# Block 0's input in 128-token halves, a split last product, gates by token in blocks 4 to 7, and block 3's statistics taken earlier

## The chip, the cores and the metric

The kernel runs on one core of one Trainium2 chip, in one launch. The metric is device time in microseconds (us), the median of several executions; before the change it is 523.41 us (three runs, 523.15 to 523.43). Each kernel also has one profiled execution, whose span is counted from its first to its last recorded instruction. In profile lines, PE is the matrix engine (TensorE), PEld its weight loads, DVE the vector engine, ACT the scalar engine, POOL the GpSimd engine, SP the sync engine, which here issues DMAs; a "q" behind a name is that engine's instruction queue.

## What is computed

The input is x, 2048 tokens of 256 channels in f32. Two sublayers stand in a sandwich: the input of each is normalised, and so is what it gives before it is added.

```python
x = x + layernorm(long_block(layernorm(x), ...))
x = x + layernorm(moe(layernorm(x), ...))

# long_block(x): 16 heads of 16 channels
h      = layernorm(x) * ln1w + ln1b
x_conv = silu(causal_depthwise_conv4(h) + conv_b)
q, k   = l2norm(h @ Wq), l2norm(h @ Wk)
v      = layernorm_per_head(h @ Wv) * vnw + vnb
i_gate = sigmoid(x_conv @ Wig + big)            # 256 wide
gamma  = sigmoid(x_conv @ Wg + bg)              # one per head, 16 wide
mem    = scan over tokens: mem[t] = gamma[t] * mem[t-1] + i_gate[t] * k[t] * v[t]
out    = groupnorm(layernorm_per_head(mem) * q) * sigmoid(x_conv @ Wog + bog)
h      = x + out @ Wo
return h + (silu(h2 @ Wgate) * (h2 @ Wval)) @ Wout      # h2 = layernorm(h), FF 1024

# moe(x): 8 experts of width 176, top 2, and a shared expert of width 704
routed + sigmoid(x @ shared_gate_w) * shared(x)
```

## The kernel before

The tokens are cut into 8 blocks of 256 (`TB`), each block into two halves of 128 tokens (`NT`), the channels into two halves of 128 (`KC`). "By token" means that tokens lie on the 128 partitions, "by channel" that channels do; PE transposes (line 380) go from one to the other. A block passes through these steps, each a small function:

- `enter` (lines 400 to 430): `enter_stats` takes bn_stats and bn_aggr of x on DVE (lines 322, 323) and on POOL `va` (line 410) and the root `inner` (line 411); `enter_norm` makes `ln_nb` on DVE (line 341) and normalises on ACT (line 343). These serve two nested norms in one. `enter_back` keeps what undoes the norm.
- `project` (lines 432 to 594): `hT` transposes the normed block and evicts it on ACT (line 447) with ln1w and ln1b as scale and bias; `conv` works as matmuls with diagonal matrices; `k`, `v` and `q` are products by token; `vscale`, `vk` finish v on DVE (lines 532 to 535, 538); `gate_in` and `gate_out` are products by channel with a tanh on ACT (line 552); `decay` is a product onto 16 rows, one for each head, a tanh, and a DMA that spreads each row over the 16 channels of its head. Every product is recorded on line 389.
- `remember` (lines 596 to 652): `scan` transposes v to channels, multiplies it by (tanh + 1) (line 606) and runs the recurrence (line 611); then `memT`, `msum`, `oscale`, `oq`, `osum`, `onorm`.
- `leave` (lines 654 to 700), `perceptron` (lines 702 to 737, 8 chunks of the hidden width, evicted on lines 724 and 725), `route` (lines 758 to 847), the shared expert (lines 854 to 882), then 36 routed blocks of 128 rows (lines 944 to 995).

Three things set the order of the work. A list written out by hand, `opening` (lines 1075 to 1087), names the steps of the first blocks one after another; each is issued behind what DVE, POOL, ACT and PE have so far. After it, `places` gives each remaining step a place, 8 places to a block, and the steps of all blocks are issued sorted by place, perceptron chunks between them. A second list by hand, `closing` (lines 1191 to 1201), orders combination, final norms and the late shared products of blocks 5 to 7; 7.6 there is the last product, of block 7's second half of tokens, and the two L steps are the two parts of `finish_last` (line 1029), whose small operations go to POOL by `scale_of` (lines 333, 334). Within the order issued, a tile scheduler places semaphores; each engine executes its own instructions in order.

PSUM is 8 banks by name: psA has two, psM three, psB, psS and psD one each (line 68). A product or a set of transposes takes one, and the next user of the bank waits until it was read.

At the start, x is loaded on SP's queue, then the weights, w_k, w_v and so on; four small rows (ln1w, ln1b, conv_b, conv_w) are loaded on ACT's queue. PE meanwhile runs ten matmuls of 512 columns on zeros (`warm_up`, line 150); two calls of `stay_warm`, six short matmuls each, stand beside hT's transposes. `vector_columns` turns the three rows into columns on PE (line 232) and a copy (line 235).

Of the kernel before, what the change touches and what calls it, by code (L numbers as in the profile page):

```python
# [27 lines left out]
def kernel(ctx: ExitStack, tc: tile.TileContext, a: dict, out: bass.AP):  # L28
# [93 lines left out]
    def load_x(b):  # L122
        x_tiles[b] = act.tile([P, NT, C], F32, tag="x", name=f"x_{b}", bufs=NB)
        nc.sync.dma_start(x_tiles[b], in_tokens(x, b))

    def in_rows(ap):
        return ap.rearrange("(k p) n -> p k n", p=P)
# [23 lines left out]

    warm_up(10)
    loads = ExitStack()
# [8 lines left out]
    nc.sync.dma_start(w_v, in_rows(a["Wv"]))  # L162
    w_io = att.tile([P, KC, 2 * C], F32, name="w_io")
    nc.sync.dma_start(w_io[:, :, 0:C], in_rows(a["Wig"]))
    head_rows = {nm: const.tile([P, D], F32, name=nm) for nm in ("vnw", "vnb", "mnw", "mnb")}
    loads.close()
    load_x(1)
    w_g = const.tile([P, KC, H], F32, name="w_g")
    nc.sync.dma_start(w_g, in_rows(a["Wg"]))
# [9 lines left out]
    nc.sync.dma_start(w_qk[:, :, 0:C], in_rows(a["Wq"]))  # L179
    nc.sync.dma_start(w_io[:, :, C:], in_rows(a["Wog"]))  # L180

# [75 lines left out]
    w_g_wide = act.tile([P, KC, C], F32, tag="f", name="w_g_wide", bufs=NB)  # L257

    wv_sum = const.tile([P, KC * H], F32, name="wv_sum")
    wv_heads = w_v.rearrange("p k (h d) -> p (k h) d", d=D)  # L260
# [55 lines left out]

    def stats(part, src):
        nt = src.shape[1]
        st = small.tile([P, nt, 6], F32, tag=f"st{part}", name="ln_st")
        mv = small.tile([P, nt, 2], F32, tag=f"mv{part}", name="ln_mv", bufs=6)  # L320
        for n in range(nt):
            nc.vector.bn_stats(st[:, n, :], src[:, n, :])  # L322
            nc.vector.bn_aggr(mv[:, n, :], st[:, n, :])  # L323
        return mv

# [74 lines left out]
    def enter(b):  # L400

        t, xt = live[b], x_tiles[b]

        def enter_stats():


            mv = stats("L", xt)
            inner = small.tile([P, NT], F32, tag="inner", name=f"inner_{b}", bufs=3)
            va = small.tile([P, NT], F32, tag="va", name=f"va_{b}", bufs=3)
            nc.gpsimd.tensor_scalar(va, mv[:, :, 1], 1.0 + EPS, EPS * EPS, ALU.mult, ALU.add)  # L410
            nc.gpsimd.tensor_tensor(inner, va, neg_half, ALU.pow)
            t.update(mv=mv, inner=inner, va=va)

        def enter_back():

            mv, inner, va = t["mv"], t["inner"], t["va"]
            outer = small.tile([P, NT], F32, tag="outer", name=f"outer_{b}")
            nc.gpsimd.tensor_scalar(outer, mv[:, :, 1], EPS, None, ALU.add)
            nc.gpsimd.tensor_tensor(outer, outer, neg_half, ALU.pow)
            back = small.tile([P, NT], F32, tag="back", name=f"back_{b}", bufs=5)  # L420
            nc.gpsimd.tensor_tensor(back, va, inner, ALU.mult)
            nc.gpsimd.tensor_tensor(back, back, outer, ALU.mult)
            t.update(back=back)

        def enter_norm():
            ln = att.tile([P, NT, C], F32, tag="ln1", name=f"ln1_{b}", bufs=4)
            normalize("L", ln, xt, t["mv"], t["inner"])
            t.update(ln=ln)

        return enter_stats, enter_back, enter_norm  # L430

    def project(b):
# [6 lines left out]
        def hT():  # L439
            hT_ = att.tile([P, KC, HALO + TB], F32, tag="hT", name=f"hT_{b}", bufs=3)  # L440
            if halo[0] is None:
                nc.gpsimd.memset(hT_[:, :, 0:HALO], 0.0)
            else:
                nc.gpsimd.tensor_copy(hT_[:, :, 0:HALO], halo[0][:, :, TB : TB + HALO])
            pt = to_channels(next(banks), t["ln"])
            for k in range(KC):
                nc.scalar.activation(
                    hT_[:, k, HALO:], pt[:, k, :], AF.Identity, bias=ln1b[k], scale=ln1w[k]
                )
            halo[0] = t["hT"] = hT_  # L450
# [86 lines left out]
        def vk():  # L537
            nc.vector.tensor_tensor(t["v"], t["v"], t["k"], ALU.mult)


# [19 lines left out]
        def decay():  # L560
# [15 lines left out]

            product(po[0:H, 0:TB], [w_g[:, k, :] for k in range(KC)], xc)
            by_head = att.tile([H, TB], F32, tag="by_head", name=f"by_head_{b}", bufs=2)
# [12 lines left out]
            values("q", w_qk[:, :, 0:C], 3), qsum, vscale, vk,  # L591
            gate("gate_in", w_io, 0, big_h, 2), decay,
            gate("gate_out", w_io, C, bog_h, 4),
        )

    def remember(b):
# [7 lines left out]
        def scan():  # L604
            u = t["gate_in"]
            nc.vector.scalar_tensor_tensor(
                u, u, 1.0, to_channels(bank, t["v"]), ALU.add, ALU.mult
            )
            mem = att.tile([P, KC, TB], F32, tag="mem", name=f"mem_{b}", bufs=2)
            for k in range(KC):  # L610
                nc.vector.tensor_tensor_scan(  # L611
                    mem[:, k, :], t["decay"][:, k, :], u[:, k, :],
                    0.0 if last[0] is None else last[0][:, k, TB - 1 : TB], ALU.mult, ALU.add,
                )
            last[0] = t["mem"] = mem
# [236 lines left out]
    all_banks = cycle("MAMDBMAS")  # L852

    def shared(b, banks=cycle("S"), shid=shid):

# [13 lines left out]
        f_ = part_of[b] if b >= LATE_FROM else new_part(b)  # L869
        for n in range(NT):  # L870
            pn = psum(next(banks))[:, 0:C]
            product(
                pn, [shid[:, f, tok(n)] for f in range(NS)], [s_down[:, f, :] for f in range(NS)],
            )
            gate = t["gate"][:, n : n + 1]
            if b < LATE_FROM:
                nc.scalar.activation(f_[:, n, :], pn, AF.Copy, scale=gate)
            else:
                nc.vector.scalar_tensor_tensor(
                    f_[:, n, :], pn, gate, f_[:, n, :], ALU.mult, ALU.add  # L880
                )
            yield
# [146 lines left out]
    def finish_last(b, n):  # L1029

        f_ = part_of[b][:, n : n + 1, :]
        mv, rs = scale_of("R", f_)
        nc.vector.tensor_scalar(f_[:, 0, :], f_[:, 0, :], mv[:, 0, 0:1], None, ALU.subtract)
        yield
# [8 lines left out]
    def evenly(n):  # L1043
# [4 lines left out]
        "hT": 0.2, "tap0": 0.3, "silu": 0.31, "k": 1.2, "ksum": 1.21, "v": 1.4, "vsum": 1.41, "vroot": 1.42, "conv": 0.3,  # L1048
        "q": 2.2, "qsum": 2.21, "vscale": 3.3, "vk": 4.3, "gate_in": 3.5, "decay": 4.5,
        "gate_out": 5.5,  # L1050
# [18 lines left out]
    for run in (  # L1069
# [11 lines left out]
        gate_in:1 qsum:1 osum decay:1 onorm gate_out:1 k:2 way_out_columns oT vroot:1 ksum:2 v:2 enter_back:1  # L1081
        h1 q:2 ln2_stats vsum:2 ln2_norm vscale:1 vk:1 conv:2 h2T enter_back:2 tables_ready
    """
# [96 lines left out]
    for b in range(LATE_FROM, NB):  # L1180
# [12 lines left out]
        6.2 N0 C2 5.6 X0 A2 6.3 A5 N1 C3 6.4 X1 A3 C6 7.0 N2 N5 C4 6.5 X2 A4 7.1 N3 X5 6.6 A6 X3 C7  # L1193
        7.2 N4 7.3 X4 N6 7.4 X6 7.5 L0 7.6 L1 L0 L1
    """
# [39 lines left out]
```

## Time and profile before

| | before |
|---|---|
| median of three runs | 523.41 us (523.15 to 523.43) |
| profiled execution | 523.42 us, its span 521.3, granted PE clock 0.996 |
| first product of k begins | 8.11 us |
| last matmul ends, last DVE operation ends | 511.48, 514.47 us |
| PE busy, 0 to 8.1 us | 5.89 us, mostly `warm_up` and `stay_warm` |
| PE busy, 60 to 65 us | 4.04 of 5 us |
| gate product onto 16 rows, blocks 4 to 7 | four records each, 0.96 us on PE |
| `gate_in` product, 8 records | 1.72 to 1.73 us on PE |

The longest waits of PE, from the trace's list of waits (engine, tile, line, whom it waited for: sum in us, times, longest):

```profile
PE psA L380 <- ACT ln L343: 1.6, 3, 1.0
PE psD L150 <- DVE cold L145: 1.2, 1, 1.2
PE psB L380 <- ACT ln L343: 0.5, 1, 0.5
PE psB L380 <- DVE o L650: 0.5, 1, 0.5
```

How to read the views below. A page gives for each engine its busy time, the share of the span and the number of instructions. A table of stretches gives for each stretch of the span its length, the busy time of PE, PEld, DVE, ACT and POOL with numbers of instructions, the granted PE clock (1.00 is full), the mean share of the 16 DMA engines and GB/s. A chain of waits is followed back from a last instruction: start, length, engine, tile and line. A timeline line gives start, busy time, engine, line, operation, out<-in, shapes and, in brackets, the idle time before it and who ended that. Matmul records are pipelined, so the busy time of a group is longer than from its start to the next group's start; a 128x256 f32 product is passed in 0.216 us a record.

### The profile page before, as it was taken

The page shows a single profiled execution, that of the slowest core. Times are in us where ns is not written, and L with a number is a line of the kernel's source. Part 1 is how long each engine was busy: PE and PEld are TensorE (multiplying, and loading weights), DVE is VectorE, ACT ScalarE, POOL GpSimd, SP SyncE. Part 2 cuts the span into 40 slices and gives each one's busy share as a digit, 9 for nine tenths or more (in the row PEclk, how much of TensorE's full clock was granted, in tenths as well). Part 3 has the DMA queues.
Part 4 walks back from the last instruction along what each step waited for, and adds up shares of the span by engine and source line. Part 5 has one row for each costly group of instructions (what it writes and reads, how often), then busy time and mean ns, then how long its engine had stood idle before and what let it go on. Part 6 is the DMA issues. An engine that isn't in the chain of part 4 may idle for free.

```text
span 521.3 us, 7930 instructions
## 1 busy us (share of the span) xinstructions
PE 505.0 (97%) x2468; PEld 421.7 (81%) x2468; DVE 331.7 (64%) x1100; ACT 217.5 (42%) x500; POOL 169.6 (33%) x309
## 2 busy tenths in 40 slices
PE   8999899999999999999999999999999999999992
PEld 5877687888888888888888888888877777778881
DVE  4788999888797896997764233235144444441983
ACT  4665463544544635643343322222134444443250
POOL 7233202213243342412426013035003443332551
PEclk9999999999999999999999999999999999999998
DMA  4991101001011011110103901003614433423621
GB/s 116 386 297 22 20 2 20 1 1 20 2 55 21 14 40 22 40 28 7 55 1 117 306 5 54 1 7 123 166 29 130 119 109 113 118 75 132 249 94 49
DMA packets 31792, 41.26 MB, mean 79 GB/s; under 512 B 4824, under 2 KB 26628, under 8 KB 31750
## 3 DMA queue, kind: packets, MB, share of 16 engines
q1 hardware_dynamic: 27888, 30.96, 20.5%
q0 software_dynamic: 3584, 9.79, 5.7%
q8 instruction: 20, 0.33, 0.3%
q14 instruction: 22, 0.18, 0.1%
q10 hardware_dynamic: 278, 0.01, 0.0%
HBM read 24.28 MB, written 15.15 MB: 76 GB/s over the span
## 4 chain that ended last, share of the span: by engine, by line
PE 82%; DVE 12%; POOL 2%; issue 1%; ACT 1%; DMA 1%; POOLq 0%; DVEq 0%
PE psM L389 35%; PE psA L389 17%; PE psD L714 9%; PE psD L389 7%; PE psS L389 5%; PE psB L389 3%; PE psA L952 2%; PE psB L980 2%; DVE ln_st L322 1%; DVE mem L611 1%; PE psB L380 1%; POOL ln_rs L334 1%; DVE hid L725 1%; DVE sm L373 1%; PE psM L380 1%
## 5 line engine op out<-in xcount | busy, mean ns | idle before, releaser
L389 PE MATMUL psM<-h2T,w_gate 128*128 128x256 f32 x256 | 66.6, 382 | 0.0
L389 PE MATMUL psM<-h2T,w_val 128*128 128x256 f32 x256 | 66.0, 379 | 0.0
L714 PE MATMUL psD<-w_out,hid 128*128 128x256 f32 x256 | 64.2, 380 | 0.1
L991 POOL DMA_INDIRECT ys<-yb,pair x36 | 35.5, 985 | 74.5 <-ACT yb L990 73.2
L389 PEld LDWEIGHTS psM<-h2T,w_gate 128*128 128x128 f32 x256 | 47.6, 190 | 8.2 <-DVE o L635 1.3
L714 PEld LDWEIGHTS psD<-w_out,hid 128*128 128x128 f32 x256 | 48.2, 190 | 7.3 <-DVE hid L725 1.0
L389 PEld LDWEIGHTS psM<-h2T,w_val 128*128 128x128 f32 x256 | 48.5, 190 | 6.5
L389 PE MATMUL psM<-m_w,xT 128*128 x144 | 48.7, 460 | 0.3 <-issue 0.3
L724 ACT ACTIVATE hid<-psM 128x256 f32<-128x256 f32 x64 | 23.8, 377 | 50.0 <-PE psM L389 49.8
L333 POOL TENSOR_SCALAR ln_rs<-ln_mv 128x2 f32<-128x2 f32 (+1 forms) x33 | 8.6, 260 | 106.5 <-DVE ln_mv L323 92.7
L725 DVE TENSOR_TENSOR hid<-hid,psM 128x256 f32<-128x256 f32 x64 | 26.1, 411 | 24.8 <-ACT hid L724 24.4
L842 POOL DMA_INDIRECT xs<-ln,rows x32 | 32.3, 1010 | 15.7 <-issue 7.2
L389 PE MATMUL psD<-m_w,hT 128*128 x144 | 37.2, 381 | 0.0
L389 PEld LDWEIGHTS psM<-m_w,xT 128*128 128x128 f32 x144 | 24.6, 190 | 8.2 <-issue 0.6
L389 PE MATMUL psA<-yT,s_gu 128*128 128x256 f32 x128 | 30.8, 381 | 0.0
L954 DVE COPY xT<-psA 128x256 f32<-128x256 f32 x36 | 15.3, 424 | 24.1 <-PE psA L952 24.1
L976 DVE TENSOR_TENSOR xb<-xb,psM 128x176 f32<-128x176 f32 x36 | 12.2, 338 | 27.0 <-ACT xb L975 17.2
L334 POOL TENSOR_TENSOR ln_rs<-ln_rs,neg_half 128x2 f32<-128x2 f32 (+1 forms) x33 | 25.8, 782 | 2.2
L389 PEld LDWEIGHTS psD<-m_w,hT 128*128 128x128 f32 x144 | 24.5, 190 | 2.4 <-ACT yb L990 0.5
L389 PEld LDWEIGHTS psA<-yT,s_gu 128*128 128x128 f32 x128 | 23.9, 190 | 3.0
L975 ACT ACTIVATE xb<-psM 128x176 f32<-128x176 f32 x36 | 11.4, 318 | 32.7 <-PE psM L389 31.8
L990 ACT ACTIVATE yb<-psD,share 128x256 f32<-128x256 f32 x36 | 17.1, 474 | 18.5 <-PE psD L389 18.4
(269 smaller groups left out, 1062.4 us busy)
## 6 DMA issues: line engine op xcount, KB each, us to landing
xb<-xs SPq DMA_DIRECT2D x36, 169.5 KB
g<-ys SPq DMA_DIRECT2D x8, 512.0 KB
xs<-zeros SPq DMA_DIRECT2D x16, 169.5 KB
x<-in_L_attn_x_dram SPq DMA_DIRECT2D x8, 256.0 KB
decay<-by_head SPq DMA_DIRECT2D x14, 128.0 KB
out_dram<-f SPq DMA_DIRECT2D x7, 256.0 KB
m_w<-in_L_ffn_w_gate_dram SPq DMA_DIRECT2D x2, 704.0 KB
m_w<-in_L_ffn_w_up_dram SPq DMA_DIRECT2D x2, 704.0 KB
```

Of the source, the lines that this page charges most:

```text
L334: roots.append(nc.gpsimd.tensor_tensor(rs, rs, neg_half[:, 0:nt], ALU.pow).ins)
L380: nc.tensor.transpose(pt[:, k * TB + n * P : k * TB + (n + 1) * P], src[:, n, k * P : (k + 1) * P], ident,)
L389: nc.tensor.matmul(po, lhs[i], rhs[i], start=(i == 0), stop=(i == len(lhs) - 1))
L714: nc.tensor.matmul(total[:, n * C : (n + 1) * C], hids[f][:, tok(n)], w_out[:, f, :], start=(f == 0 and n == 0), stop=(f == NF - 1 and n = ...
L724: nc.scalar.activation(hid, po[:, 0:TB], AF.Silu)
L725: nc.vector.tensor_tensor(hid, hid, po[:, TB:], ALU.mult)
L842: inst = nc.gpsimd.indirect_dma_start(out=xs, out_offset=bass.IndirectOffsetOnAxis(ap=rows[:, c : c + 1], axis=0), in_=ln[:, n, :], in_off ...
L954: nc.vector.tensor_copy(xT, pt[:, 0 : KC * P].rearrange("p (k t) -> p k t", k=KC))
L975: nc.scalar.activation(h[:, 0:I], po[:, 0:I], AF.Silu)
L976: nc.vector.tensor_tensor(h[:, 0:I], h[:, 0:I], po[:, I:GU], ALU.mult)
L990: nc.scalar.activation(yb, po[:, 0:C], AF.Copy, scale=share)
L991: inst = nc.gpsimd.indirect_dma_start(out=ys, out_offset=bass.IndirectOffsetOnAxis(ap=pair, axis=0), in_=yb, in_offset=None, bounds_check= ...
```

## The change

- Block 0's x is loaded as two DMAs of 128 tokens, the first on SP's queue, the second on ACT's queue (ahead of the four small rows). Its statistics, `va`, `inner`, `ln_nb`, norm, transposes and eviction go half by half; of the evictions, channel half 0 stays on ACT and channel half 1 goes to DVE. `warm_up` runs nine matmuls instead of ten.
- `w_io` holds Wig, Wg and Wog side by side. For blocks 4 to 7, `gate_in` is a product by token, 272 columns wide, of Wig and Wg together: the convolved tokens are the stationary side. ACT copies it out of two psA banks, DVE adds the row `big` (loaded over all partitions at the start), ACT takes the tanh. `vk` then multiplies by (tanh + 1) by token, so `scan` reads the transposed product straight from PSUM. `decay` transposes the 16 columns of Wg's part to 16 rows instead of making a product. The places of `gate_in` and `decay` go from 3.5 to 3.8 and from 4.5 to 5.0 in all blocks.
- `enter_stats` of block 3 leaves its place and goes into `opening`, between `vscale:1` and `vk:1`.
- In `closing`, the last product is made in two halves of 128 output channels, each evicted and taken into bn_stats by itself. For both halves of tokens, `finish_last` adds epsilon on DVE instead of POOL; the root stays on POOL.

On each engine this moves, beside the operations named: on POOL, block 0's `va` and `inner` become four operations on one column each, in the order va, va, inner, inner; on ACT, the DMAs of conv_b and conv_w wait for the semaphores of the two x halves; on PE, block 0's transposes fill a psA and a psM bank.

```diff
     def load_x(b):
         x_tiles[b] = act.tile([P, NT, C], F32, tag="x", name=f"x_{b}", bufs=NB)
-        nc.sync.dma_start(x_tiles[b], in_tokens(x, b))
+        if b > 0:
+            nc.sync.dma_start(x_tiles[b], in_tokens(x, b))
+        else:
+            for n, queue in enumerate((nc.sync, nc.scalar)):
+                queue.dma_start(x_tiles[b][:, n, :], in_tokens(x, b)[:, n, :])
...
-    warm_up(10)
+    warm_up(9)
...
-    w_io = att.tile([P, KC, 2 * C], F32, name="w_io")
+    w_io = att.tile([P, KC, 2 * C + H], F32, name="w_io")
...
-    w_g = const.tile([P, KC, H], F32, name="w_g")
+    w_g = w_io[:, :, C : C + H]
...
+    BY_TOKEN = tuple(range(4, NB))
+    big_row = act.tile([P, NT, C], F32, tag="f", name="big_row", bufs=NB)[:, 0, :]
+    nc.sync.dma_start(big_row, a["big"].partition_broadcast(P))
...
         def enter_stats():
-            mv = stats("L", xt)
             inner = small.tile([P, NT], F32, tag="inner", name=f"inner_{b}", bufs=3)
             va = small.tile([P, NT], F32, tag="va", name=f"va_{b}", bufs=3)
-            nc.gpsimd.tensor_scalar(va, mv[:, :, 1], 1.0 + EPS, EPS * EPS, ALU.mult, ALU.add)
-            nc.gpsimd.tensor_tensor(inner, va, neg_half, ALU.pow)
+            def root(ns, mv):
+                nc.gpsimd.tensor_scalar(
+                    va[:, ns], mv[:, ns, 1], 1.0 + EPS, EPS * EPS, ALU.mult, ALU.add
+                )
+                nc.gpsimd.tensor_tensor(inner[:, ns], va[:, ns], neg_half[:, ns], ALU.pow)
+            if b > 0:
+                mv = stats("L", xt)
+                root(slice(0, NT), mv)
+            else:
+                mv = stats("L", xt, lambda n, mv: root(slice(n, n + 1), mv))
...
         def enter_norm():
-            normalize("L", ln, xt, t["mv"], t["inner"])
+            for ns in [slice(0, NT)] if b > 0 else [slice(n, n + 1) for n in range(NT)]:
+                normalize("L", ln[:, ns, :], xt[:, ns, :], t["mv"][:, ns, :], t["inner"][:, ns])
...
+                for n in range(NT):
+                    pt = psum(next(banks))
+                    for k in range(KC):
+                        nc.tensor.transpose(pt[:, tok(k)], t["ln"][:, n, tok(k)], ident)
+                    to = slice(HALO + n * P, HALO + (n + 1) * P)
+                    nc.scalar.activation(
+                        hT_[:, 0, to], pt[:, tok(0)], AF.Identity, bias=ln1b[0], scale=ln1w[0]
+                    )
+                    nc.vector.tensor_scalar(
+                        hT_[:, 1, to], pt[:, tok(1)], ln1w[1], ln1b[1], ALU.mult, ALU.add
+                    )
...
         def vk():
             nc.vector.tensor_tensor(t["v"], t["v"], t["k"], ALU.mult)
+            if b in BY_TOKEN:
+                nc.vector.scalar_tensor_tensor(t["v"], t["gate_in"], 1.0, t["v"], ALU.add, ALU.mult)
+
+        def gate_in():
+            g = att.tile([P, NT, C + H], F32, tag="gate_in", name=f"gate_in_{b}", bufs=2)
+            for n in range(NT):
+                po = psum(next(banks))
+                product(
+                    po[:, 0 : C + H], [t["xc"][:, k, tok(n)] for k in range(KC)],
+                    [w_io[:, k, 0 : C + H] for k in range(KC)],
+                )
+                nc.scalar.copy(g[:, n, :], po[:, 0 : C + H])
+            t["heads"], g = g[:, :, C:], g[:, :, 0:C]
+            nc.vector.tensor_tensor(g, g, big_row.unsqueeze(1).to_broadcast([P, NT, C]), ALU.add)
+            nc.scalar.activation(g, g, AF.Tanh, scale=0.5)
+            t["gate_in"] = g
...
-            product(po[0:H, 0:TB], [w_g[:, k, :] for k in range(KC)], xc)
+            if b in BY_TOKEN:
+                for n in range(NT):
+                    nc.tensor.transpose(po[0:H, tok(n)], t["heads"][:, n, :], ident)
+            else:
+                product(po[0:H, 0:TB], [w_g[:, k, :] for k in range(KC)], xc)
...
         def scan():
-            u = t["gate_in"]
-            nc.vector.scalar_tensor_tensor(
-                u, u, 1.0, to_channels(bank, t["v"]), ALU.add, ALU.mult
-            )
+            u = to_channels(bank, t["v"])
+            if b not in BY_TOKEN:
+                g = t["gate_in"]
+                nc.vector.scalar_tensor_tensor(g, g, 1.0, u, ALU.add, ALU.mult)
+                u = g
...
+    def halves(b, n):
+        whole = 2 if (b, n) == (NB - 1, NT - 1) else 1
+        return [slice(j * C // whole, (j + 1) * C // whole) for j in range(whole)]
...
     def finish_last(b, n):
-        mv, rs = scale_of("R", f_)
-        nc.vector.tensor_scalar(f_[:, 0, :], f_[:, 0, :], mv[:, 0, 0:1], None, ALU.subtract)
+        for j, c in enumerate(parts):
+            nc.vector.bn_stats(st[:, j, :], f_[:, 0, c])
+            if j < len(parts) - 1:
+                yield
+        nc.vector.bn_aggr(mv, st)
+        nc.vector.tensor_scalar(rs, mv[:, 1:2], EPS, None, ALU.add)
+        nc.gpsimd.tensor_tensor(rs, rs, neg_half[:, 0:1], ALU.pow)
+        nc.vector.tensor_scalar(f_[:, 0, :], f_[:, 0, :], mv[:, 0:1], None, ALU.subtract)
...
-        "q": 2.2, "qsum": 2.21, "vscale": 3.3, "vk": 4.3, "gate_in": 3.5, "decay": 4.5,
+        "q": 2.2, "qsum": 2.21, "vscale": 3.3, "vk": 4.3, "gate_in": 3.8, "decay": 5.0,
...
-        h1 q:2 ln2_stats vsum:2 ln2_norm vscale:1 vk:1 conv:2 h2T enter_back:2 tables_ready
+        h1 q:2 ln2_stats vsum:2 ln2_norm vscale:1 enter_stats:3 vk:1 conv:2 h2T enter_back:2 tables_ready
...
-        7.2 N4 7.3 X4 N6 7.4 X6 7.5 L0 7.6 L1 L0 L1
+        7.2 N4 7.3 X4 N6 7.4 X6 7.5 L0 7.6 L1 7.7 L1 L0 L1
```

## The prediction

> **What bounds the kernel now.** I began with the page's busy shares, then went to busy time by stretch, and only then to single waits. The page:
>
> ```profile
> PE 505.0 (97%) x2468; PEld 421.7 (81%) x2468; DVE 331.7 (64%) x1100; ACT 217.5 (42%) x500; POOL 169.6 (33%) x309
> ```
>
> TensorE (PE) works 505.0 of 521.3 us, so only two things shorten the run: fewer PE microseconds, or less of the 16.3 us in which PE stands still. The table of stretches (length, then busy time of PE, weight loads, DVE, ACT, POOL) says where the latter lie:
>
> ```profile
> 0.00:8.10 8.10, 5.89 (x28) 2.69 (x28) 3.54 (x13) 3.19 (x6) 5.30 (x21) 1.00 0.56 165
> 8.10:20.00 11.90, 11.89 (x55) 10.13 (x56) 8.60 (x28) 6.67 (x13) 5.07 (x11) 1.00 0.70 251
> ...
> 60.00:65.00 5.00, 4.04 (x24) 3.15 (x22) 4.12 (x16) 2.31 (x6) 2.10 (x6) 1.00 0.11 15
> ...
> 110.00:120.00 10.00, 10.00 (x48) 8.11 (x48) 9.93 (x31) 4.00 (x9) 1.15 (x3) 1.00 0.00 1
> ...
> 260.00:382.00 122.00, 121.55 (x593) 107.20 (x592) 44.49 (x190) 34.10 (x84) 33.02 (x58) 1.00 0.28 83
> ```
>
> PE is full from 8.1 on except for a hole of 0.96 in 60 to 65; DVE is as full as PE in 110 to 120, where the first gate by token falls. The last matmul ends at 511.48, so the head (8.1 us, of which 5.89 busy are mostly warm-ups on zeros) and the tail (9.8 us) have no PE work to hide them. Their chains (start, length, what):
>
> ```profile
> 0.74 2.73 DMA x<-in_L_attn_x_dram
> 3.49 0.75 DVE ln_st L322 x2
> 4.24 0.23 DVE ln_mv L323 x2
> 4.82 0.72 POOL inner L411
> 6.27 0.59 ACT ln L343
> 8.11 2.02 PE psM L389 x8
> ```
> ```profile
> 509.31 2.17 PE psM L389 x10
> 511.50 0.50 DVE f L879
> 512.90 0.30 POOL ln_rs L333
> 513.24 0.73 POOLq L1231
> 513.99 0.48 DVE f L1035
> ```
>
> Every piece waits for the one above it. The hole and the decay product, from the timeline:
>
> ```profile
> 63.36 0.33 PE L380 MATMUL psA<-ident,ln 128*128 128x128 f32 x1 [0.96 <-ACT ln L343]
> 111.77 1.89 PE L389 MATMUL psA<-xc,w_io 128*128 128x256 f32 x8
> 116.62 1.04 PE L389 MATMUL psA<-xc,w_g 128*16 128x256 f32 x4
> 117.58 1.13 PE L389 MATMUL psM<-h2T,w_gate 128*128 128x256 f32 x4
> ```
>
> **Part 1, block 0 in halves.** The transfer stays at 256 KB. Before: x lands 3.47, both bn_stats to 4.24, both aggr to 4.47, POOL va and inner to 5.54, nb, two ACT norms of 0.59 (0.50 apart) to 6.86, transposes, six stay-warm matmuls 0.50, two hT evictions to 8.51; k starts at 8.11 but takes 2.02 instead of 8 x 0.216 = 1.73, so it counts as starting at 8.23 (its two waits give back 0.16 elsewhere; I take 8.2). After, the half that decides is the second. DVE still runs bn, bn, aggr, aggr, since both halves land together: aggr 1 at about 4.25 to 4.45. POOL runs va 0, va 1, inner 0, inner 1 one after another on one column each; a one-column form is not in this stretch, the nearest rows are the tail's 0.30 and 0.57 to 0.73, so inner 1 ends at about 6.1, later than 5.54. ACT norm 1 then runs about 6.33 to 6.92 (before 6.86): nothing gained there. The gain is behind it: only two transposes are left then (0.33), and hT runs beside stay-warm as two 128-column evictions on ACT and DVE, against 1.02 on ACT alone. Transposes end at 7.25, stay-warm at 7.75, k starts there: 8.2 - 7.75 = **-0.45**, bounds -1.0 (norm 1 not delayed) and +0.2 (POOL serial time worth 0.9 instead of 0.57).
>
> What is pushed: the two row DMAs conv_b and conv_w stand on ACT's queue behind the lanes of the x halves, so they start at about 3.5 instead of 1.7 and 2.0. Behind them on ACT are the norms, not due before 5.3. The rows land, at the 2.0 us of the bog row's issue, at about 5.6, so PE's transposes of the rows move from 5.17 to 5.6; with stay-warm they end by 6.4, before the first half's norm needs PE. POOL's big and bog DMAs (0.78, 0.52) and diagonals (6.88 to 9.76) move 0.6 later, to about 10.4; the convolution reads them at about 11.2. DVE's weight centring ends near 9.05; v starts at about 9.5. These cost nothing while those margins of 0.5 to 0.8 hold. The extra DMA of the big row on SP is issued among the weights and has 100 us.
>
> A rule speaks against this part. The Trainium skill, "DMA: Bandwidth & Descriptors", section "Issuing engines are not separate DMA queues", says that transfers from several issuing engines interleave on the same 16 engines and a second issuer saves only issue time. Row: x took 2.73, and the next 256 KB (w_k), queued right behind, were there 0.69 later, so bytes are the small part. By the rule both halves land at 3.47, as summed. If the first half came half of 0.69 = 0.35 earlier, bn 0 would run before bn 1's data are there, and the part be worth about -0.6.
>
> A second: "TensorE: Matmul & The Clock Gate", section "What's actually happening", has the PE start at half rate and open after a busy window of about 3.4 us that runs free. Rows: ten warm-ups took 4.03 us, 0.40 each, and the records after them are quick (six in 0.51). Nine last 3.6, still above 3.4, but then PE idles from 4.85 to 5.6, where before it idled not at all. By the rows alone it costs 0; if the window is missed, one more window at half rate costs an estimated 1.7. I take 0 and give the 1.7 a tenth.
>
> **Part 2, gates by token, blocks 4 to 7.** Removed per block: the decay product, four records 116.62 to 117.58 = 0.96. These load only 16 columns of weights, yet cost as much as full records. Added: two transposes to 16x128 (four of 128x128 take 0.44 to 0.60; two 0.22 to 0.30, I take 0.32 with their turn-around), and 16 columns more on each of gate_in's 8 records: 128x256 costs 0.216, so 0.0135 a column-16, 8 x 0.0135 = 0.11. Net -0.96 + 0.32 + 0.11 = -0.53, and four times **-2.1**. Lower bound if transposes cost 0.22: -2.5.
>
> Off PE, per block: DVE gains the big_row add and a (g+1)v (0.68 to 0.69 each, row L533) and loses the scan's (0.68, L606): +0.69. ACT: before 2 x 0.47 tanh; now two copies of 128x272 (0.35 each, from half of 0.57 for 128x512) and one 128x512 tanh of about 0.63: +0.4 to +0.65. New waits: (a) the copy must free psA before the second bank's user; q's copy ends at 112.26 and the second bank is needed about 112.69, margin 0.43. (b) ACT's tanh now waits for a DVE add, and hid, norm and evictions queue behind it in ACT's order. The order lists put the big_row add behind the ln_nb that feeds the zero-slack transpose at 120.28, and ln_2 ahead of hid, so I see no PE wait there; DVE's idle gaps of 1.08 at 124.74 and 1.75 at 130.91 take the surplus. If a bank or tanh came late all the same, each would cost PE what it is late beyond 0.43. Bounds -2.5 and, if each addition comes back as a wait, 0 (further is the rival below).
>
> **Part 3, block 3's statistics** move before vk:1, which DVE runs at 51.48, about 8 us earlier, so the 0.96 before 63.36 goes: DVE ran bn at 58.98, POOL's inner ended at 62.48, ACT's norm began at 62.71. What is late next: the same DVE work (2 bn, 2 aggr, 1.2 us) now lies ahead of block 1's scan, memory and o, and DVE is 4.9 to 5.0 of 5 full in 50 to 60. Waits on o and ln of 0.45 (at 78.38 and 88.42) show how such lateness surfaces. I let nearly a half come back: **-0.55**, bounds -1.3 (following waits shrink also) and +0.5 (the 1.2 us all falls on PE).
>
> **Part 4, the tail.** Before, from 511.50 to 514.47, the seven pieces run one after another. Now the last half product leaves eviction and bn on 128 columns (about 0.30 and 0.25: -0.39), and the 0.30 add moves to DVE at about 0.15 to 0.20 (-0.1 with one hand-over). PE's 10 records of 256 become 20 of 128 at about 0.114 (s_gu 128x137 records take 0.12), +0.1 to +0.24. **-0.35**, bounds -0.6 and +0.1.
>
> **Sum.** -0.45 - 2.1 - 0.55 - 0.35 = -3.45. The profiled execution took 523.42 (span 521.3 and 2.1 around it), 0.01 over the median 523.41: no correction. 523.4 - 3.45 = **519.95**, -0.66%. A measurement of this kernel tells about 0.2% (1.05 us) from no change.
>
> **Rivals.**
> - *The gates' PE saving comes back as waits* on DVE or on the second psA bank. For: DVE 9.93 of 10 in 110 to 120. Against: DVE's busy share falls to 7.90 and 7.86 of 10 in the two stretches behind it, so a queue of 0.69 is worked off before the next block. 523.4 - 0.45 - 0.55 - 0.35 = 522.05. Chance 0.13.
> - *The clock stays at half through the opening*: 519.95 + 1.7 = 521.65. Against: 3.6 us of warm-up. Chance 0.10.
> - *Slower: tanh in ACT's queue.* The in-order ACT waits in gate_in for DVE's add, which itself stands behind up to two 0.68 operations of a saturated DVE; behind tanh stand hid and the norms that PE needs next. Two DVE operations and the add itself are 2.1 us per block. PE's cover is one perceptron chunk pair, about 1 us; from a PE wait of 0.53 + 0.34 = 0.87 per block on (the other parts' 1.35 spread over four blocks is 0.34) nothing is left; at 1.3 per block the time is 522.05 + 4 x (1.3 - 0.53) = 525.1. For: the 0.43 margin. Against: the ACT order. Chance 0.10 of slower by over 0.2%, as far as 525.
> - *Halves that don't act as halves*: POOL's four serial operations eat the head, and part 3's stall only moves: 519.95 + 0.45 + 0.55 = 520.95. Chance 0.17.
> - The forecast itself: 0.50, own range 518.7 to 520.9.
>
> Range: 518.6 to 522.8; the slower rival and a sum of all lower bounds (517.9) lie outside. Faster by over 0.2% takes the forecast, the moved stall, the clock and two thirds of the first rival, 0.50 + 0.17 + 0.10 + 0.05; I round to 0.80. Same 0.10, slower 0.10.
>
> **What would show it.** Right: k's first product at 7.6 to 7.9; no PE wait over 0.3 before the transpose of block 3's ln; in blocks 4 to 7 no four 16-column records, PE busy down by about 2 to 2.5; last DVE operation about 3 - 0.5 after the last matmul. Wrong: PE waits of 0.5 or more on psA in gate_in, on a tanh, or on o around 115 to 235; half-rate records after 7 us; psS rows after 6.4. A DVE that falls behind all through blocks 4 to 7 would break the sum.

## The result, and the profile after

The change takes 523.82 us (median of 20 executions, 522.58 to 526.51), the kernel before 523.27 (20 executions, 522.98 to 523.55): a ratio of 1.0016, 95% interval [1.0009, 1.0023]. Forecast was 519.95. Two things want an explanation: 3.9 us that did not come, and that the executions now lie 3.9 us apart, where before it was 0.6.

The profiled execution has a span of 521.6 us against 521.3. Its engines, from the page:

```profile
PE 505.0 (97%) x2469; PEld 423.0 (81%) x2469; DVE 335.1 (64%) x1111; ACT 217.8 (42%) x504; POOL 173.3 (33%) x309
```

PE is as busy as before to a tenth, although four products of 0.96 us each were taken out; DVE has 3.4 us more and POOL 3.7. The stretches (columns as before):

```profile
0.00:8.10 8.10, 5.91 (x23) 3.03 (x24) 1.79 (x9) 2.94 (x5) 4.82 (x22) 1.00 0.59 165
8.10:20.00 11.90, 11.90 (x57) 10.24 (x56) 10.39 (x31) 6.03 (x12) 5.44 (x12) 1.00 0.68 239
60.00:65.00 5.00, 5.00 (x29) 4.41 (x28) 5.00 (x15) 3.06 (x7) 0.53 (x1) 1.00 0.40 51
120.00:130.00 10.00, 9.53 (x48) 7.84 (x47) 9.62 (x39) 6.61 (x17) 5.03 (x13) 1.00 0.15 20
```

The hole of 60 to 65 is closed. But 120 to 130, where PE had been busy 9.97 of 10 and DVE 7.90, now has 9.53 and 9.62: DVE's surplus did not drain behind the gate. The row of that stretch before the change:

```profile
120.00:130.00 10.00, 9.97 (x52) 8.44 (x51) 7.90 (x37) 5.71 (x15) 4.69 (x13) 1.00 0.19 25
```

PE's waits name the rest (sum in us, times, longest):

```profile
PE psM L400 <- ACT yT L823: 1.3, 4, 0.7
PE psS L677 <- DVE mem L667: 1.0, 2, 0.7
PE psS L238 <- POOL hT L463: 1.0, 1, 1.0
```

**The head.** PE and ACT's queue in the kernel before:

```profile
5.17 0.28 PE L232 MATMUL psS<-ident,setup 3*128 3x3 f32 x2
5.39 0.51 PE L150 MATMUL psD<-cold 128*128 128x128 bf16 x6
9.96 1.89 PE L389 MATMUL psA<-w_v,hT 128*128 128x256 f32 x8
1.69 0.27 ACTq L156 DMA_DIRECT2D setup<-in_L_attn_conv_b_dram  x1
```

And in the change, first PE, then ACT's queue:

```profile
6.21 0.34 PE L238 MATMUL psS<-ident,setup 3*128 3x3 f32 x2 [0.97 <-POOL hT L463]
6.49 0.82 PE L155 MATMUL psD<-cold 128*128 128x128 bf16 x6
8.59 2.55 PE L400 MATMUL psA<-w_qk,hT 128*128 128x256 f32 x8
10.98 1.89 PE L400 MATMUL psM<-w_v,hT 128*128 128x256 f32 x8
```
```profile
3.60 0.23 ACTq L161 DMA_DIRECT2D setup<-in_L_attn_conv_b_dram  x1
3.87 0.40 ACTq L163 DMA_DIRECT2D conv_w<-in_L_attn_conv_w_dram  x1
```

conv_b's DMA is issued at 3.60 instead of 1.69: in the trace it waits for the semaphore of the x half on ACT's own queue, and conv_w's DMA for that of the other half; DVE begins on x at 3.44. The transposes of the rows come at 6.21 instead of 5.17, and PE stands still for 0.97 before them. The releaser named, a clearing of hT's margin on POOL, feeds nothing of theirs; the rows do. And the six stay-warm matmuls behind them take 0.82, where they took 0.51: they are passed at half rate. The weight loads tell it too: they stand 0.43 us apart in k's product until 9.9, and 0.22 from there on (in the kernel before the records are at full rate from 5.4 on). The clock column says 1.00 in both profiles, so it does not show this. k starts at 8.59, v at 10.98 instead of 9.96: the head is 1.02 longer, not 0.45 shorter.

**The gates.** Block 4 in the kernel before, behind its gate product at 111.77:

```profile
119.05 0.15 DVE L341 SCALAR_TENSOR_TENSOR ln_nb<-ln_mv,ln_rs 128x2 f32<-128x2 f32 x1
120.23 0.56 ACT L767 COPY yT<-psM 128x512 f32<-128x512 f32 x1
120.28 0.65 PE L380 MATMUL psB<-ident,ln 128*128 128x128 f32 x4
120.96 1.17 PE L389 MATMUL psM<-s_gu,yT 128*128 128x137 f32 x8
```

And in the change:

```profile
112.45 2.00 PE L400 MATMUL psA<-w_io,xc 128*128 128x272 f32 x8
117.31 0.38 PE L630 MATMUL psA<-ident,gate_in 128*16 128x128 f32 x2
119.18 0.15 DVE L352 SCALAR_TENSOR_TENSOR ln_nb<-ln_mv,ln_rs 128x2 f32<-128x2 f32 x1
119.37 1.09 ACT L354 ACTIVATE ln<-h,ln_nb,ln_rs 128x256 f32<-128x256 f32 x2 [4.50 <-DVE ln_nb L352]
120.63 0.57 ACT L823 COPY yT<-psM 128x512 f32<-128x512 f32 x1
121.25 1.20 PE L400 MATMUL psM<-s_gu,yT 128*128 128x137 f32 x8 [0.19 <-ACT yT L823]
129.05 0.75 DVE L781 TENSOR_TENSOR hid<-hid,psM 128x256 f32<-128x256 f32 x2
129.52 1.99 PE L770 MATMUL psD<-w_out,hid 128*128 128x256 f32 x8 [0.16 <-DVE hid L781]
```

Measured from the start of gate_in's product, the transposes of the norm begin after 8.51 us before (111.77 to 120.28) and after 7.67 now (112.45 to 120.12): PE has saved 0.84, more than the 0.53 of the sum. The router's product s_gu, yT begins after 9.19 before, 8.80 now: 0.45 is given back, because the norm stood in ACT's queue until DVE's ln_nb came at 119.18 (119.05 before, so DVE hardly moved). The copy yT (the router's input by channel), which could have been made from 117.5 on, stood behind the norm while ACT had nothing to do for 4.50. The w_gate product behind w_out (130.71 before, 131.35 now) begins after 18.94 and 18.90: the rest went on hid, the perceptron's hidden values, which DVE finished late. In block 7 the wait for yT alone is 0.71.

**The tail.** The last pieces, from the timeline:

```profile
511.18 1.28 PE L400 MATMUL psD<-s_down,shid 128*128 128x128 f32 x10
512.49 0.35 DVE L940 SCALAR_TENSOR_TENSOR f<-psD,gate,f 128x128 f32<-128x128 f32 x1
512.88 0.29 DVE L1098 BATCH_NORM_STATS2 ln_st<-f 128x6 f32<-128x128 f32 x1
513.45 0.15 DVE L1102 TENSOR_SCALAR ln_rs<-ln_mv 128x1 f32<-128x1 f32 x1
513.68 0.58 POOL L1103 TENSOR_TENSOR ln_rs<-ln_rs,neg_half 128x1 f32<-128x1 f32 x1 [1.41 <-DVE ln_rs L1102]
513.78 1.01 DVE L1106 SCALAR_TENSOR_TENSOR f<-f,ln_rs,x 128x256 f32<-128x256 f32 x2
```

The last products start 0.92 later than before (510.06 against 509.14), and the last DVE operation ends only 0.31 later (514.79 against 514.47): the tail gains 0.6.

### The profile page after: what moved, and what is told of

Its sections match the earlier page's. It is cut to its first block, busy times and chain, and to the rows that moved or that the text cites. A ratio compares the mean times of both kernels' runs of the same rounds, so it can differ in the third digit from the quotient of the medians.

```text
span 521.6 us, 7952 instructions
## 1 busy us (share of the span) xinstructions
PE 505.0 (97%) x2469; PEld 423.0 (81%) x2469; DVE 335.1 (64%) x1111; ACT 217.8 (42%) x504; POOL 173.3 (33%) x309
## 4 chain that ended last, share of the span: by engine, by line
PE 63%; DVE 28%; POOL 3%; ACT 2%; issue 2%; DMA 1%; POOLq 0%; DVEq 0%
PE psM L400 26%; PE psA L400 11%; PE psD L400 7%; PE psD L770 6%; PE psS L400 5%; DVE xc L498 3%; DVE ln_st L332 2%; PE psB L400 2%; DVE hid L781 2%; PE psA L1013 2%; PE psB L1041 2%; POOL ln_rs L345 1%; DVE ss L384 1%; DVE o L372 1%; DVE sm L384 1%
## 5 line engine op out<-in xcount | busy, mean ns | idle before, releaser
L344 POOL TENSOR_SCALAR ln_rs<-ln_mv 128x2 f32<-128x2 f32 x31 | 8.3, 269 | 101.8 <-DVE ln_mv L333 86.7
L345 POOL TENSOR_TENSOR ln_rs<-ln_rs,neg_half 128x2 f32<-128x2 f32 x31 | 25.0, 808 | 2.0
```

The source lines that it names most:

```text
L345: roots.append(nc.gpsimd.tensor_tensor(rs, rs, neg_half[:, 0:nt], ALU.pow).ins)
```

## The experiments

**Part 1: which half of the head costs.** `one_load` undoes only the second DMA, `no_head` the whole part; `head_only` is the part alone.

```diff
 one_load
...
-            for n, queue in enumerate((nc.sync, nc.scalar)):
-                queue.dma_start(x_tiles[b][:, n, :], in_tokens(x, b)[:, n, :])
+        nc.sync.dma_start(x_tiles[b], in_tokens(x, b))
```

> The change with block 0's x loaded by one DMA on SP again; half-by-half statistics, norms and evictions and the nine warm-ups stay. Theory A (the second x DMA takes the turn of a row DMA, conv_b and conv_w wait for x, PE idles 0.97 us before the rows' transposes and runs on at half rate): the rows are back at about 5.2 us, PE does not idle there, v's product starts at or before 9.9 instead of 10.98, and the time falls by 1.0 to 1.5 us to about 522.5, with the runs within 0.6 us of each other instead of 3.9. Rival B (nine warm-ups are too few for the clock, whatever the rows do): the time stays near 523.8 and the runs stay spread over 2 us or more. Rival C (POOL's four one-column operations and the half evictions are what is slow): the time stays near 523.8, but the spread is narrow.

> The change without its first part (one DMA of x, block 0 in one piece, ten warm-ups); gates by token, block 3's statistics and the split last product stay. Theory A: the head's +1.02 us of the profile goes: about 522.7 us, narrow runs. If the head is not the cause of the loss (the gates are, by waits of ACT and DVE): 523.8 as before, and the runs stay spread.

> The kernel before with the first part alone (the wider w_io and the load of the big row stay, unused by the gates). Theory A: 523.3 + 1.0 = about 524.3 us, with runs spread over 2 us or more. As predicted on record: 523.3 - 0.45 = 522.85.

`one_load`: 522.62 us (522.38 to 524.45), ratio to before 0.999 [0.9982, 0.9999]; `no_head`: 522.74 (522.6 to 523.58), 0.9993 [0.9985, 1.0001]; `head_only`: 524.98 (523.7 to 528.11), 1.0038 [1.0023, 1.0054]. So the part costs 1.1 in the change and 1.6 alone, and the spread comes with it. Theory A holds for the rows: in `one_load` their transposes are back at 5.17. But 4 of its 13 executions still lie between 523.79 and 524.45, so that they spread over 2 us, as rival B had it, and the profiled one is among the late ones. PE's timeline of it:

```profile
5.17 0.37 PE L233 MATMUL psS<-ident,setup 3*128 3x3 f32 x2
5.47 0.82 PE L150 MATMUL psD<-cold 128*128 128x128 bf16 x6
8.16 3.09 PE L395 MATMUL psA<-w_qk,hT 128*128 128x256 f32 x8
```

The rows are on time, and the records are at half rate all the same, until 10.4. So both theories held something, and three more kernels take the warm-ups apart: thirteen in the change, ten with one DMA, nine in the kernel before (`warm_up(13)`, `warm_up(10)`, `warm_up(9)`).

> The change with thirteen warm-ups instead of nine, which fills PE until the late rows are there (6.2 us); all else stays. Theory A, clock part: the records behind them run at full rate (six stay-warm in 0.5 instead of 0.82 to 0.85, k in 1.73 to 2.0 instead of 2.34), the executions lie within 0.8 us instead of 3.9, and the time falls to about 523.0; the lateness of the rows, 0.3 to 0.6 us, stays. If the head's loss is the rows' lateness alone: 523.8, spread as before.

> The change with one DMA of x and ten warm-ups; block 0 still goes half by half. Theory A with both of its parts (the rows' turn, and a clock that opens late when PE is not busy for long enough): no half-rate records after 5.4 us, runs within 1 us, and k at 7.6 to 7.9: 522.74 (the change without its first part) - 0.3 = about 522.4 or a little less. If half by half is itself no gain (POOL's four operations): 522.7. If ten is no better than nine: a third of the runs stay at 523.8 to 524.5.

> The kernel before with nine warm-ups instead of ten and nothing else. If the clock opens only after PE was busy for long enough in a window that runs free: most executions at 523.3, and some (one_load had 4 of 13) at 1.2 to 2 us more. If the count is no matter: all within 523.0 to 523.6.

`warm13`: 523.2 (522.39 to 524.16), 0.9999 [0.999, 1.0007]; full rate (six stay-warm in 0.51), k at 8.37. Its spread of 1.8 is half of the change's but not the 0.8 expected, and 0.6 against the version with one DMA remains: its rows' transposes come at 6.87, behind the thirteen warm-ups. `one_load_w10`: 522.63 (522.32 to 523.24), 0.9987 [0.998, 0.9994]. `before_warm9`: 523.69 (523.3 to 526.39), 1.002 [1.0011, 1.0029]; 10 of its 22 executions lie between 524.6 and 526.4, against one (525.91) of the 245 of the kernel before that were measured beside the change and these runs. So the tenth warm-up alone decides whether hardly any or nearly half of the executions come late. That a late execution is one at half rate is seen in `one_load`'s profile; the profiled execution of `before_warm9` was a quick one (523.3) and shows full rate. With one DMA and ten warm-ups, PE's timeline is this:

```profile
4.99 0.51 PE L150 MATMUL psD<-cold 128*128 128x128 bf16 x6
7.54 1.95 PE L395 MATMUL psA<-w_qk,hT 128*128 128x256 f32 x8
9.68 1.56 PE L395 MATMUL psM<-w_v,hT 128*128 128x256 f32 x6 [0.19 <-DVE w_v L270]
```

k starts at 7.54, 0.57 before the old 8.11; v, which waits for its weights, starts at 9.68 against 9.96. So half by half gains 0.28 in the trace, where 0.45 was forecast. In the medians it is 0.11 (522.63 against `no_head`'s 522.74), within their intervals.

**Part 2: the gates.** `gates_only` is the part alone; `half_decay` saves PE time at the same place by leaving out half of a contraction, and changes nothing on the other engines; `gates_nodve` leaves out the two new DVE operations.

```diff
 half_decay (on the kernel before)
-            product(po[0:H, 0:TB], [w_g[:, k, :] for k in range(KC)], xc)
+            ks = range(1) if b >= 4 else range(KC)
+            product(po[0:H, 0:TB], [w_g[:, k, :] for k in ks], [xc[k] for k in ks])
 gates_nodve (on gates_only)
-            nc.vector.tensor_tensor(g, g, big_row..., ALU.add)
...
-                nc.vector.scalar_tensor_tensor(t["v"], t["gate_in"], 1.0, t["v"], ALU.add, ALU.mult)
 gates_yt (on gates_only), the router's places
-        (route, 4, (1.4, 2.0, 4.2, 5.2, 5.3, 9.2, 10.2, 10.3)),
+        (route, 4, (1.4, 2.0, 3.5, 5.2, 5.3, 9.2, 10.2, 10.3)),
```

> The kernel before with the gates by token of blocks 4 to 7 alone. Theory D (each block's 0.95 us saved on PE comes back within 13 us, as waits for ACT's norm and yT, which stand behind DVE's ln_nb, and for DVE's hid): within 0.3 us of before, 523.0 to 523.6. As predicted on record: 523.3 - 2.1 = 521.2. Rival E (the saving is real and the head's shift alone hides it): below 522.2.

> The kernel before, but in blocks 4 to 7 the product onto 16 rows takes only the first half of the channels (it leaves the other half of the contraction out): two of its four PE records go, 0.48 us a block, and no other engine has anything more or less to do. Theory D1 (at this place PE is no longer alone on the critical path: the norm for the transposes at 120.28 ends when DVE's queue has come to its ln_nb, so PE's saving turns into a wait there): within 0.4 us of before, and in the trace a wait of 0.3 to 0.5 us on ACT's norm at psB in each of the four blocks. Rival D2 (the place is PE's, and what costs in the change is the work added on DVE and ACT): 4 x 0.48 = 1.9 us faster, about 521.5.

> The gates by token alone, without their two new operations on DVE: the add of the big row and the product with (tanh + 1) are left out, so DVE has 0.68 us less a block than in the kernel before instead of 0.69 more. D2: the waits for DVE's hid at 129 and part of the waits for the norm go: 2 to 3 us below the gates alone (524.35), about 521.8. D1: the waits on the norm and on yT before 122 stay, because ln_nb stands ahead of both operations in DVE's queue; only the wait at 129 goes (0.35 a block): about 523.0.

> The gates by token alone, with the third step of the router (the transposes to yT and their copy) at place 3.5 instead of 4.2, so that ACT's copy of yT runs ahead of the norm of ln2 and not behind it; nothing is added or left out. If the waits of the shared and router products for yT (0.19, 0.19, 0.19 and 0.71, and up to 0.27 more in each block behind the late norm) come from ACT's order: 1.3 us below the gates alone, 523.0 to 523.3. If yT is late because of DVE's norm behind it in any case: 524.3.

`gates_only`: 524.35 (524.19 to 525.31), 1.0022 [1.0014, 1.003]: not even, but 0.95 slower. `half_decay`: 522.34, 0.998 [0.9973, 0.9988]: 1.03 of 1.92 stays, between D1 and D2. Where it stays is seen when the start of the same product on PE is compared with the kernel before (us, + is later):

| product, its start in the kernel before | `half_decay` | `gates_only` | `gates_yt` |
|---|---|---|---|
| w_qk ahead of block 4's gates, 105.72 | +0.04 | +0.11 | 0.00 |
| w_qk behind block 4's gates, 135.48 | +0.01 | +0.58 | +0.39 |
| w_qk behind block 5's gates, 171.73 | -0.20 | +0.87 | +0.60 |
| w_qk behind block 6's gates, 207.98 | -0.44 | +1.15 | +0.83 |
| last product onto w_o, 278.52 | -0.91 | +0.87 | -0.59 |

Of the 0.48 that `half_decay` takes from each block, 0.03 stays in block 4, 0.21 and 0.24 in blocks 5 and 6, and 0.47 in block 7 and behind it. ACT's norm and its copy yT begin no earlier than before (119.25 and 120.25 in block 4, 155.35 and 156.35 in block 5), so PE only reaches them sooner. D1 is right for block 4, D2 for block 7, and each by half for the two between.

`gates_nodve`: 522.57, 0.9987 [0.998, 0.9994], 1.8 below `gates_only` and between D1's 523.0 and D2's 521.8: the waits for hid are gone, those of 0.19 for yT remain. `gates_yt`: 523.01, 0.9991 [0.9983, 1.0]: 1.34 below, as expected, with no wait for yT left. By the table it still loses in blocks 4, 5 and 6 (0.39, 0.21 and 0.23) and gains 1.4 in block 7 and behind it; gates by token in block 7 alone were not tried. The loss in the three blocks is at hid, behind one scaling of o in DVE's queue:

```profile
128.19 0.69 DVE L701 TENSOR_TENSOR o<-o,rm 128x512 f32<-128x512 f32 x1
128.80 0.75 DVE L776 TENSOR_TENSOR hid<-hid,psM 128x256 f32<-128x256 f32 x2
129.27 0.92 PE L765 MATMUL psD<-w_out,hid 128*128 128x256 f32 x3 [0.54 <-DVE hid L776]
```

Two attempts to relieve DVE failed, and both tell something. `nohead_yt_pool` puts the add on POOL (`nc.gpsimd` in the place of `nc.vector`); `gates_yt_os` lets ln_nb run ahead of two operations on o (`"oscale": 11.1` becomes 11.7); `before_yt_os` is its control without the gates.

> A version that should beat both: the change without its first part, with the yT step at 3.5, and with the add of the big row on POOL instead of DVE. D2 (the added DVE work is what the gates cost, with ACT's order): 522.74 - 1.3 for yT - 0.5 to -1.5 for the add = 520.0 to 521.0, and no wait for hid at 129, 165 and 202 (0.55 each with yT early). If POOL's add delays the root of ln2 behind it instead: waits for the norm grow at 120, and the time is 521.4 or more.

> The gates by token alone, with yT at 3.5 as in gates_yt and the scaling of o (oscale) at place 11.7 instead of 11.1, which lets ln_nb of ln2 run ahead of two 0.68 us operations in DVE's queue; no work is added or left out. If the place of ln_nb in DVE's queue sets the wait at 120: the waits for the norm in psB go, blocks 4 to 7 keep 0.3 to 0.6 us more each than in gates_yt (523.01): 521.0 to 522.2. If DVE's load as a whole sets it: the wait moves on to hid at 129 and grows there, and the time stays within 0.3 of 523.0.

> The kernel before with the same two places (yT at 3.5, oscale at 11.7) and nothing else: the control. PE had no wait at 120 before, so nothing is to be gained: 523.0 to 523.4. If it falls by more than 0.5, the gain of gates_yt and gates_yt_os is that of the places and not of the gates' cover.

`nohead_yt_pool`: 523.14, 1.0 [0.9991, 1.0008], 0.4 worse than `no_head`, although the yT step was moved as well. Its timeline:

```profile
116.40 1.79 POOL L582 TENSOR_TENSOR gate_in<-gate_in,big_row 128x512 f32<-128x512 f32 x1
116.99 1.75 DVE L564 TENSOR_TENSOR k<-k,rkv 128x512 f32<-128x512 f32 x1
119.27 0.15 DVE L347 SCALAR_TENSOR_TENSOR ln_nb<-ln_mv,ln_rs 128x2 f32<-128x2 f32 x1
120.10 0.33 PE L386 MATMUL psB<-ident,ln 128*128 128x128 f32 x1 [0.80 <-ACT ln L349]
```

The add takes 1.79 on POOL instead of 0.67, and the DVE operation beside it 1.75 instead of 0.68, so DVE lost more than it was spared, and ACT's norm behind ln_nb, and PE behind that, came late. In each of the four blocks PE waits 0.68 to 0.80 there.

`gates_yt_os`: 526.05, 1.005 [1.0037, 1.0063]; `before_yt_os`: 524.44, 1.0021 [1.0014, 1.0028]. The waits on the norm went, and came back larger at hid:

```profile
130.62 0.74 DVE L776 TENSOR_TENSOR hid<-hid,psM 128x256 f32<-128x256 f32 x2
131.09 1.13 PE L765 MATMUL psD<-w_out,hid 128*128 128x256 f32 x4 [1.84 <-DVE hid L776]
```

The control has such a wait once, 1.36 in block 3 (at 94.80), and none in blocks 4 to 7; with the gates it is 1.84, 1.39 and 1.38 in blocks 4 to 6. So the wait moves on to hid and grows, as the rival had it, but the rival's time, within 0.3 of 523.0, is missed by 3.0: DVE's load between two hid operations counts, and two more operations on o were put into just that stretch. The control's 1.0 was not expected; it is that one wait. Behind it the two moves alone gain nothing: at the three products w_qk of the table the control is 1.0 later each time.

**Parts 3 and 4 alone.**

> The kernel before with block 3's statistics in the opening alone. As the milestones of the runs so far have it (perceptron of block 1 reached 0.38 us earlier with this part than without it): 523.3 - 0.4 = 522.9, the wait of 0.96 before block 3's transposes gone and a wait of about 1.0 on DVE's scan before memT of block 1 in its place. As on record: -0.55. Rival F (with the gates as they were, the place at 120 gives all of it back): 523.3.

> The kernel before with the split last product and the add on DVE alone. As on record -0.35; as the trace of the change has it (last matmul +0.92 to last DVE operation +0.31 against before) -0.6: 522.7 to 523.0. If only the time to the last DVE operation falls and the two output DMAs, now issued together, take it back: 523.3.

`stats_only`: 522.52, 0.9986 [0.9979, 0.9993], -0.77; the 0.96 before block 3's transposes is gone, and one wait for block 1's scan is new, as said (a second one, 0.26, was 0.25 before):

```profile
56.49 0.30 PE L672 MATMUL psS<-ident,mem 128*128 128x128 f32 x1 [0.74 <-DVE mem L662]
```

At first this gives PE almost nothing: the wait for the norm at 88 grows from 0.45 to 0.75, and the transposes behind it begin at 88.34 against 88.42. The gain comes later, between 90 and 132 us: block 4's ln_nb is made at 118.24 instead of 119.05, and the next norm's transposes begin at 131.76 instead of 132.44. DVE is busy 18.00 of the 18 us from 60 to 78, where it had 17.09, so that the hole had been one of DVE too; that DVE's lead is what pays is read from these rows, and no run isolates it. `tail_only`: 522.66, 0.9988 [0.9981, 0.9994], -0.63.

**Put together.**

> All that is known put together: the change with one DMA of x and ten warm-ups, yT at 3.5 and oscale at 11.7. one_load_w10 had 522.63; the gain of yT was 1.34 on the gates, and that of oscale 0 to 2: 519.5 to 521.3.

> The change with one DMA of x, ten warm-ups and yT at 3.5 (oscale stays at 11.1). 522.63 (one_load_w10) less the 1.34 that yT gave on the gates alone: about 521.3. If the waits on hid at 129, 165 and 202 grow as in gates_yt and more, 522.0 or above.

> The change with one DMA of x, ten warm-ups and without the gates by token: half-by-half block 0, block 3's statistics and the split last product remain. 523.35 - 0.77 - 0.63 = 521.95 from the two parts alone; half by half adds -0.1 to -0.4: about 521.7.

`best1` (with the oscale move): 524.19, 1.0015 [1.0009, 1.0022], a miss for the reason just shown. `best4`, the change with one DMA, ten warm-ups and no gates: 522.06, 0.9975 [0.9966, 0.9984]. `best3`, with the gates and yT at 3.5: 521.47 (521.12 to 522.3), 0.9964 [0.9951, 0.9978], 1.9 below before and 2.3 below the change. The gates cost 0.57 without the move of yT (522.63 against 522.06) and are worth 0.59 with it, though from five executions, and the intervals of `best3` and `best4` overlap. Here too PE loses 0.32, 0.20 and 0.23 against `best4` behind the gates of blocks 4 to 6, and the gain lies in block 7 and behind it. `best4` with yT at 3.5 was not run; that this move needs the gates to be worth anything rests on the control above.

## Why the prediction was wrong

**Part 1** (forecast -0.45, measured +1.1 in the change): two terms were put at nothing. The first failed step is "These cost nothing while those margins of 0.5 to 0.8 hold". The wait of conv_b and conv_w was seen, with their landing at 5.6; PE got the rows at 6.2, 2.6 us after their issue, where 2.0 had been taken from another row, and the margin of 0.5 was used up. The second is the clock: "I take 0 and give the 1.7 a tenth". It was valued by one execution of the kernel before. The Trainium skill, "TensorE: Matmul & The Clock Gate", section "What's actually happening", says that the window of about 3.4 us is free-running and the onset varies from run to run. Nine warm-ups exceed that window (3.84 us at the 0.43 of the weight loads; the prediction's 3.6 took 0.40 each), and still 10 of 22 executions of `before_warm9` were late. The scatter fits the page; why ten are enough and nine are not, no run shows. A single profile that ran well is one draw of such a thing; the spread should have been in the forecast. The halves themselves were right in sign: without the two costs they gave 0.28 in the trace, not 0.45.

**Part 2** (forecast -2.1, measured +0.57 beside the other parts, +0.95 alone), which is most of the miss: the PE term was sound, even too small (0.84 in block 4 against 0.53). The step that failed is "so I see no PE wait there; DVE's idle gaps of 1.08 at 124.74 and 1.75 at 130.91 take the surplus". In `gates_only` PE waits for yT in every block (0.19 to 0.71) and for hid in three (0.16 to 0.17). The zero-slack place was named, but its meaning was not drawn: where PE arrives just as ACT's norm and yT are ready, PE coming earlier gains nothing unless they come earlier too, and `half_decay` shows that in block 4 without a single added operation. The gap at 124.74 stood before hid, so a surplus that used it up made hid late. The first rival (the saving comes back as waits) was right in kind with a chance of 0.13; it named DVE, but at its other suspect, the second psA bank, PE never waited, and ACT's order with yT behind the norm was not thought of. It also stopped at zero, while the added DVE work (1.8, `gates_only` against `gates_nodve`) costs more than what PE saves without it (0.8). The slower rival looked at ACT's queue, but at the tanh: it is issued behind yT (121.46), and ahead of the norm ACT stood idle.

**Part 3** (-0.55, measured -0.77): the sign and nearly the size were right, the path only in part. The hole went and a wait on block 1's scan took its place, as forecast, but by 88 us nearly all of it had come back, not a half; the gain appears behind that, where DVE is ahead.

**Part 4** (-0.35, measured -0.63) was right in mechanism. The mis-sized term is the eviction and statistics on half the channels together with the add: from last matmul to last DVE operation it is 2.3 us instead of 3.0.

Alone the four parts measure +1.6, +0.95, -0.77 and -0.63, which sums to +1.15 with before at about 523.3; the change has +0.55. They do not add: beside the others the gates cost 0.57 instead of 0.95, and the head 1.1 instead of 1.6. Two slips in the prediction's sums change nothing of this: all lower bounds together give 518.0, not 517.9, and two thirds of the first rival's 0.13 are 0.09, not 0.05.

## What to carry to other kernels

Where the bounding engine arrives at a place just in time, without a wait, look at what else arrives there: a saving on that engine is worth only what the others have in hand, and taking away some of its work without touching theirs tells that in one run. Look at each repetition by itself: here the same edit lost in three blocks and gained in the fourth. Before adding an operation to a second engine that is full, find the next instruction in its queue that the first engine waits for. And work that only keeps a clock up has to be judged by many executions, not by one profile.

## What the runs showed of the hardware

Half-rate products stand in a profile whose granted-clock column says 1.00; only the spacing of weight loads (0.43 against 0.22) and the longer executions tell of it. One more DMA at the start delayed two others by nearly 2 us (conv_b from 1.69 to 3.60, conv_w from 1.99 to 3.87), since each now waits for a semaphore that an x half holds; with one DMA they are back at 1.70 and 2.00. A 128x512 f32 add took 1.79 on POOL against 0.67 on DVE, and the DVE operation beside it took 1.75 instead of 0.68.
